# Which of two streams of matmul pieces goes on while a PSUM bank is half used, inside a state-space loop

## The chip, the cores and the metric

The kernel runs on one core of a Trainium2 chip. A core has five engines with queues of their own: TensorE (PE in the profile, with PEld for its weight loads), VectorE (DVE), ScalarE (ACT), GpSimd (POOL) and SyncE (SP), which here issues most DMAs. Matmuls write to PSUM, a small memory of eight banks; the other engines work mostly in SBUF. Each engine runs its own instructions in a fixed order, and waits on semaphores for the others. The metric is device time in microseconds; a kernel that computes the same in less time is better.

## The reference

A two-layer network on x of 64 sequences, 64 positions and 256 features, with a conditioning vector for each sequence. Each layer is a conditioning block, a mixing block, a second conditioning block and a feed-forward block, with two residual additions. The change touches the mixing block of the second layer, a selective state-space model, and what runs beside it, the shared experts and the router of the next block:

```
xz = x @ W_in;  xi, z = split(xz)                      # 512 + 512 channels
xc = silu(causal_conv4(xi) + b_conv)
delta_lr, B, C = split(xc @ W_xproj, [16, 32])         # 16 states
delta = softplus(delta_lr @ W_dt + b_dt);  A = -exp(A_log)
h_t = exp(delta * A) * h_(t-1) + delta * B * xc        # for each channel and state
y_t = sum over states of h_t * C + D * xc
x   = x + (y * silu(z)) @ W_out
...
shared = sum over 2 experts of (silu(x @ s_w1.T) * (x @ s_w3.T)) @ s_w2.T
scores = sigmoid([x, t_emb] @ W_router.T);  top 2 of 8 routed experts
```

Everything is float32.

## The kernel before

The kernel is one program for one core, written in Python against a layer that records the instructions, schedules them by priority and places the semaphores. The order in which the Python code issues an instruction is its priority; an instruction that asks for a buffer of a pool that has none free is put behind the one that frees it.

The 4096 tokens are handled in eight chunks of 512 (`CH`), each of eight sequences. Features lie on partitions, tokens along the free dimension. The state-space block is the function `mamba`. Its 512 channels are four tiles of 128 partitions, taken two at a time (`PI = 2`), and the 16 states are taken one after the other. So a chunk has 2 x 16 = 32 steps (`STEPS`), and the loop `for s in range(LAST)` has 256 steps. One step is, for one state and 2 x 512 columns:

- POOL: `hb = dx * B` (L1046, in `inputs`), issued two steps ahead. There are five `hb` buffers, and B comes by a broadcast DMA (L993) for two states at a time.
- ScalarE: the decay `dA = exp(A * delta)` (L1053, in `decay`), two instructions, issued one step ahead. There are three `dA` buffers, in PSUM.
- TensorE: `cb` (L998, in `spread_c`), which copies the row of C to all partitions; one PSUM bank.
- VectorE: two scans over time (L1094), which turn `hb` into the state, and a product with `cb` (L1096).
- TensorE: eight transposes (L1109) that add the 16 states up in two PSUM banks `yp0` and `yp1`.

Beside these steps runs all other work of the block, cut into pieces by Python generators:

- `head(c + 1)`: the input projection, convolution and delta of the next chunk (L919, L923, L926, L930, L934, L958 to L972).
- `gates(c, i0)`: the projection of z and its Silu (L982, L985, L988). In each tile the two halves of the sum over features are two pieces.
- `finish`: the transposes back (L1006, L1008, L1009).
- `project(c)`: the output projection (L1023, four matmuls for each of two tiles, in pairs), the residual addition that reads the bank (L1026), the load and the store of x (L1016, L1028). Its last act is to hand the new x to `beside`.
- `beside(c)`: router scores and shared experts of the next block for chunk c (L1499 to L1515, L1820 to L1842), up to 56 pieces a chunk. They use a bank of their own, `mq`.

The first four ask for one PSUM bank, `mp`, of which there is one during the loop. A generator that stops while it is in the middle of filling the bank yields `MID`; at the end of a use it yields nothing (`None`). Two streams stand in line: `urgent` (the `finish` and `project` of the chunk just scanned) and `pieces` (gates and the next chunk's head):

```
pieces = chain(pieces, gates(c, now, 0), islice(ahead, 3 * NI + PI + 4), gates(c, now, PI), ahead)
...
urgent = chain(urgent, finish(c, now, p * PI, yT))
if j == STEPS - 1:
    urgent = chain(urgent, project(c, now))
```

The function `turn` hands out one piece. It is called 40 times a chunk (`LEFT`), and more often where the next chunk's delta is needed sooner. After it, each step takes its share of `beside`. The `project` of a chunk runs in the first steps of the next one, where `pieces` begins with that chunk's gates.

On ScalarE the exponential, the logarithm and Silu need different function tables. Where two instructions that follow each other need different ones, a table load stands between them; it has the line of the instruction that needs it.

After the loop comes the stage of the routed experts (`mixtures`), with the rest of the shared experts for the last chunk.

Of the kernel before, what the change touches and what calls it, by code (L numbers as in the profile page):

```python
# [857 lines left out]
MID, END = "mid", "end"  # L858


def mamba(g, w, hs, beside):
# [16 lines left out]
    with (  # L878
# [97 lines left out]
        def gates(c, v, i0):  # L976
            sz = p2.tile([P, PI, CH], F32, name="sz")
            v.sz.append(sz)
            for i in range(PI):
                ps = one()  # L980
                for k in range(KD):
                    nc.tensor.matmul(ps, w.Win[:, k, ts(NI + i0 + i, P)], hs2[:, k, ts(c, CH)], start=(k == 0), stop=(k == KD - 1))  # L982
                    if k == 0:
                        yield MID
                nc.scalar.copy(sz[:, i, :], ps)  # L985
                if i < PI - 1:
                    yield
            nc.scalar.activation(sz, sz, AF.Silu)  # L988
            yield
# [11 lines left out]
        def finish(c, v, i0, yT):  # L1001

            for i in range(PI):
                ps = one()
                for t in range(CH // P):
                    nc.tensor.transpose(ps[:, ts(t, P)], yT[i][:, t, :], g.ident)  # L1006
                y = v.xc[:, i0 + i, :]
                nc.vector.scalar_tensor_tensor(y, y, w.col[:, 2, i0 + i : i0 + i + 1], ps, ALU.mult, ALU.add)  # L1008
                nc.gpsimd.tensor_mul(y, y, v.sz[i0 // PI][:, i, :])  # L1009
                yield  # L1010

        def project(c, v):

            nonlocal others
            x = p2.tile([P, KD, CH], F32, name="x")
            nc.sync.dma_start(x, g.x[:, :, ts(c, CH)])  # L1016

            to = x if c + 1 < NCH else hs2[:, :, :CH]
            yield
            for k in range(KD):  # L1020
                ps = one()
                for i in range(NI):
                    nc.tensor.matmul(ps, w.Wout[:, i, ts(k, P)], v.xc[:, i, :], start=(i == 0), stop=(i == NI - 1))  # L1023
                    if i % 2 and i < NI - 1:
                        yield MID
                nc.vector.tensor_add(to[:, k, :], x[:, k, :], ps)  # L1026
                yield
            nc.sync.dma_start(g.x[:, :, ts(c, CH)], to)  # L1028
            if c + 1 < NCH:
                for _ in others:  # L1030
                    pass
                others = beside(c, x)
# [36 lines left out]
        urgent, pieces, others = iter(()), iter(()), iter(())  # L1069
        mid = None  # L1070

        def turn():

            nonlocal mid
            got = next(pieces, None) if mid else next(urgent, END)
            if got is END:
                got = next(pieces, None)
            mid = got

        for s in range(LAST):  # L1080
            c, j = divmod(s, STEPS)
# [2 lines left out]
            if j == 0:  # L1084
                ahead = head(c + 1, vs[c + 1]) if c + 1 < NCH else iter(())
                pieces = chain(pieces, gates(c, now, 0), islice(ahead, 3 * NI + PI + 4), gates(c, now, PI), ahead)
# [11 lines left out]
            if s + AHEAD < LAST:  # L1098
                ca, ja = divmod(s + AHEAD, STEPS)
                while vs[ca].ready <= ja // S * PI:  # L1100
                    turn()
                inputs(s + AHEAD)
# [15 lines left out]
            if n == S - 1:  # L1118
# [3 lines left out]
# [3 lines that stand above are left out]
            while left < (j + 1) * LEFT // STEPS:  # L1125
                left += 1
                turn()
# [1061 lines left out]
```

## Time and profile before

| what | time, us |
|---|---|
| median of 3 runs | 2806.84 (2806.24 to 2814.49) |
| the profiled execution | 2807.03 |
| its span, first to last instruction | 2804.6 |
| before the state loop (0 to 698.5) | 698.5 |
| state loop (698.5 to 1849.1) | 1150.6 |
| after it | 955.5 |

Busy time over the whole span is 2339.3 us on PE, 1770.7 on DVE, 1375.5 on ACT and 1340.5 on POOL. In the state loop alone PE is busy for 924.1, DVE for 1013.0, ACT for 736.8 and POOL for 868.5 of the 1150.6 us.

In the profile each group of instructions is a line of the kernel, an engine, an operation, the tiles written and read, and a shape. "Idle before" is the time in which that engine did nothing before these instructions, and the name after the arrow is what ended it. A float32 matmul of the program shows as two instructions in the trace. Lines are those of the kernel before; in the changed kernel everything after `turn` stands four lines lower. The state loop's steps are counted from 0 in each chunk, and chunks from 0.

### The profile page before, as it was taken

The page shows a single profiled execution, that of the slowest core. Times are in us where ns is not written, and L with a number is a line of the kernel's source. Part 1 is how long each engine was busy: PE and PEld are TensorE (multiplying, and loading weights), DVE is VectorE, ACT ScalarE, POOL GpSimd, SP SyncE. Part 2 cuts the span into 40 slices and gives each one's busy share as a digit, 9 for nine tenths or more (in the row PEclk, how much of TensorE's full clock was granted, in tenths as well). Part 3 has the DMA queues.
Part 4 walks back from the last instruction along what each step waited for, and adds up shares of the span by engine and source line. Part 5 has one row for each costly group of instructions (what it writes and reads, how often), then busy time and mean ns, then how long its engine had stood idle before and what let it go on. Part 6 is the DMA issues. An engine that isn't in the chain of part 4 may idle for free.

```text
span 2804.6 us, 34388 instructions
## 1 busy us (share of the span) xinstructions
PE 2339.3 (83%) x11977; PEld 1674.0 (60%) x11996; DVE 1770.7 (63%) x2980; ACT 1375.5 (49%) x2289; POOL 1340.5 (48%) x1166
## 2 busy tenths in 40 slices
PE   3989967996568888887978888687786989999995
PEld 3634436773345555554655555566664768888884
DVE  0477748973999898888889797852353442322333
ACT  0567528885466757584757676533232222222220
POOL 0022345521696868685878787835555331111110
PEclk9979988997769999998999999899998999999997
DMA  9999820002112122221121222325685755555655
GB/s 224 372 358 347 276 70 1 1 1 90 68 68 83 65 74 70 72 72 57 65 92 67 83 81 75 106 70 178 212 287 194 278 216 206 214 192 197 227 192 189
DMA packets 180501, 406.03 MB, mean 145 GB/s; under 512 B 24785, under 2 KB 84434, under 8 KB 174946
## 3 DMA queue, kind: packets, MB, share of 16 engines
q1 hardware_dynamic: 166882, 366.80, 38.4%
q0 software_dynamic: 13440, 36.98, 3.4%
q8 instruction: 96, 1.57, 0.2%
q14 instruction: 83, 0.68, 0.1%
HBM read 280.76 MB, written 144.98 MB: 152 GB/s over the span
## 4 chain that ended last, share of the span: by engine, by line
PE 43%; DVE 21%; ACT 13%; issue 9%; POOL 5%; another core or an unknown queue 2%; DMA 1%; DVEq 0%; SPq 0%; ACTq 0%; POOLq 0%
DVE hb L1094 12%; PE ps L1684 11%; PE acc L1582 8%; PE out L450 4%; DVE hb L1096 3%; ACT dA L1053 2%; PE ps L1651 2%; PE yp L1109 2%; PE mq L1820 1%; DVE xc L926 1%; PE s L416 1%; PE acc L441 1%; ACT L1053 1%; PE mp L982 1%
## 5 line engine op out<-in xcount | busy, mean ns | idle before, releaser
L1046 POOL TENSOR_TENSOR hb<-dx,Bn 128x1024 f32<-128x1024 f32 x256 | 606.4, 2377 | 269.0 <-PE yp L1109 219.7
L1094 DVE TENSOR_TENSOR_SCAN hb<-dA,hb 128x512 f32<-128x512 f32 x512 | 602.1, 1210 | 63.2 <-ACT dA L1053 59.8
L1053 ACT ACTIVATE dA<-delta,negA 128x504 f32<-128x504 f32 x512 | 345.6, 685 | 303.5 <-DVE hb L1094 298.3
L1109 PEld LDWEIGHTS yp<-ident,hb 128*128 128x128 f32 x2048 | 264.4, 150 | 160.2 <-issue 121.2
L1096 DVE TENSOR_TENSOR hb<-hb,cb 128x1024 f32<-128x1024 f32 x256 | 312.4, 1220 | 66.3 <-PE cb L998 48.0
L1684 PE MATMUL ps<-gxT,w 128*128 128x256 f32 (+1 forms) x1600 | 324.5, 361 | 1.2 <-DVE gxT L1559 0.8
L1684 PEld LDWEIGHTS ps<-gxT,w 128*128 128x128 f32 x1600 | 276.3, 190 | 47.2 <-issue 12.4
L1820 PE MATMUL mq<-x,moe_s 128*128 128x256 f32 x896 | 244.5, 405 | 66.1 <-ACT up L1827 29.9
L1109 PE MATMUL yp<-ident,hb 128*128 128x128 f32 x2048 | 298.6, 290 | 0.0
L1358 POOL DMA_INDIRECT ffn_y<-gy,to x72 | 69.2, 962 | 432.3 <-ACT gy L1584 419.8
L1820 PEld LDWEIGHTS mq<-x,moe_s 128*128 128x128 f32 x896 | 166.6, 200 | 131.7 <-ACT sh L1824 42.5
L1688 DVE TENSOR_TENSOR gh<-gs,ps 128x256 f32<-128x256 f32 (+1 forms) x200 | 78.6, 394 | 213.5 <-ACT gs L1687 206.2
L1582 PE MATMUL acc<-w,gh 128*128 128x256 f32 (+1 forms) x864 | 190.0, 390 | 0.0
L1584 ACT ACTIVATE gy<-acc,wt 128x256 f32<-128x256 f32 x152 | 67.4, 474 | 246.8 <-PE acc L1582 227.5
L1687 ACT ACTIVATE gs<-ps 128x256 f32<-128x256 f32 (+1 forms) x200 | 72.4, 364 | 235.4 <-PE ps L1684 219.3
L998 PE MATMUL cb<-parts,pick 80*128 80x512 bf16 x256 | 104.5, 408 | 88.2 <-DVE hb L1096 83.9
L1582 PEld LDWEIGHTS acc<-w,gh 128*128 128x128 f32 (+1 forms) x864 | 146.8, 191 | 30.4 <-issue 13.2
L432 POOL TENSOR_TENSOR E<-E,z 128x1024 f32<-128x1024 f32 x32 | 61.6, 1925 | 194.5 <-DVE z L431 118.0
L1358 POOL DMA_INDIRECT moe_y<-gy,to x80 | 78.0, 975 | 110.2 <-ACT gy L1584 91.3
L1582 PE MATMUL acc<-w,rh 128*128 128x256 f32 x320 | 88.5, 419 | 45.6 <-ACT rh L1653 40.3
L1572 DVE TENSOR_REDUCE wt<-pick 128x2 f32<-128x4 f32 (+1 forms) x88 | 13.6, 156 | 174.7 <-ACT gy L1584 164.0
L450 PE MATMUL out<-oT,hs 128*128 128x512 f32 x256 | 117.8, 604 | 1.5 <-ACT oT L443 1.5
(470 smaller groups left out, 4457.1 us busy)
## 6 DMA issues: line engine op xcount, KB each, us to landing
w<-ffn_w SPq DMA_DIRECT2D x40, 2176.0 KB
Bn<-B SPq DMA_DIRECT2D x128, 512.0 KB
moe_x<-fill SPq DMA_DIRECT2D x130, 260.0 KB
ffn_x<-fill SPq DMA_DIRECT2D x129, 260.0 KB
w<-moe_w SPq DMA_DIRECT2D x48, 512.0 KB
ffn_w<-in_ffn_W_dram SPq DMA_DIRECT2D x16, 640.0 KB
gx<-moe_x SPq DMA_DIRECT2D x32, 260.0 KB
gx<-ffn_x SPq DMA_DIRECT2D x32, 260.0 KB
```

Of the source, the lines that this page charges most:

```text
L450: nc.tensor.matmul(ps, M[:, o, ts(k, P)], v.o[:, o], start=(o == 0), stop=(o == H // 2 - 1))
L998: nc.tensor.matmul(t, pick[:, n : n + 1].to_broadcast([rows, P]), v.parts, start=True, stop=True)
L1046: nc.gpsimd.tensor_mul(hb, vs[c].dx[p], Bn[:, n % NB, :].unsqueeze(1).to_broadcast([P, PI, CH]))
L1053: nc.scalar.activation(decays[s][i][:, :, 1:], seq(vs[c].delta[p][:, i, :])[:, :, 1:], AF.Exp, scale=A[:, p * PI + i, n : n + 1],)
L1094: ins = nc.vector.tensor_tensor_scan(h, dA[i].rearrange("p b l -> p (b l)"), h, 0.0, ALU.mult, ALU.add)
L1096: ins = nc.vector.tensor_tensor(hb, hb, cb.unsqueeze(1).to_broadcast([P, PI, CH]), ALU.mult)
L1109: nc.tensor.matmul(yp[i][:, t, :], hb[:, i, ts(t, P)], g.ident, start=(n == 0 and t == 0), stop=(n == S - 1 and t == CH // P - 1), is_tran ...
L1358: i = self.g.nc.gpsimd.indirect_dma_start(out=self.y, out_offset=bass.IndirectOffsetOnAxis(ap=to, axis=0), in_=y, in_offset=None)
L1582: nc.tensor.matmul(po[s], h, w, start=(i == 0), stop=(i == n - 1))
L1684: nc.tensor.matmul(ps[:, j, :], v.w12[:, k, ts(j * (full + 1) + i, P)], v.xT[:, k, :], start=(k == 0), stop=(k == KD - 1))
L1688: nc.vector.tensor_mul(v.h[:, i, : v.rows], s, ps[:, 1, :])
L1820: nc.tensor.matmul(ps[:, i % 2, :], w[:, k, ts(i, P)], xu[:, k, :], start=(k == 0), stop=(k == KD - 1))
```

## The change

Only `turn` is changed. Before, it remembered what the last piece had yielded: after a `MID`, from either stream, the next piece came from `pieces`. After, it remembers the stream itself: after a `MID` the next piece comes from the stream that yielded it.

```diff
@@ -1072,10 +1072,14 @@
         def turn():
 
             nonlocal mid
-            got = next(pieces, None) if mid else next(urgent, END)
-            if got is END:
-                got = next(pieces, None)
-            mid = got
+            if mid is None:
+                mid = urgent
+            got = next(mid, END)
+            if got is END and mid is urgent:
+                mid = pieces
+                got = next(mid, END)
+            if got is not MID:
+                mid = None
```

`MID` is the string "mid" and `END` the string "end". The two differ where `urgent` yields `MID`, which only `project` does, once for each of its two tiles.

## The prediction

> **What bounds the kernel now.** I read the page first, then the stretches of the state loop by chunk, then VectorE's waits inside that loop, then the order of time around the longest of them. Of the page, the span and three groups:
>
> ```profile
> span 2804.6 us, 34388 instructions
> L1094 DVE TENSOR_TENSOR_SCAN hb<-dA,hb 128x512 f32<-128x512 f32 x512 | 602.1, 1210 | 63.2 <-ACT dA L1053 59.8
> L1053 ACT ACTIVATE dA<-delta,negA 128x504 f32<-128x504 f32 x512 | 345.6, 685 | 303.5 <-DVE hb L1094 298.3
> L1096 DVE TENSOR_TENSOR hb<-hb,cb 128x1024 f32<-128x1024 f32 x256 | 312.4, 1220 | 66.3 <-PE cb L998 48.0
> ```
>
> The scan and its product are the state loop. VectorE's idle time before them has two main releasers: ScalarE's decay (59.8 us) and TensorE's row copy of C, `cb` (48.0). By stretches (us, then busy time and count of PE, PEld, DVE, ACT, POOL, the granted clock, DMA):
>
> ```profile
> core 0: us, PE busy (x) PEld busy (x) DVE busy (x) ACT busy (x) POOL busy (x), PEclk, DMA share, GB/s
> ...
> 1113.60:1256.60 143.00, 123.02 (x574) 82.80 (x573) 124.69 (x118) 96.46 (x132) 108.44 (x53) 0.96 0.21 71
> 1256.60:1414.60 158.00, 125.89 (x556) 82.88 (x555) 135.76 (x151) 98.60 (x133) 107.92 (x56) 0.89 0.18 61
> ...
> 1849.10:1869.30 20.20, 18.94 (x73) 12.48 (x73) 2.87 (x4) 2.50 (x5) 7.33 (x27) 1.00 0.27 83
> 1869.30:2804.60 935.30, 828.42 (x4077) 683.27 (x4077) 337.13 (x1372) 223.74 (x524) 260.26 (x290) 0.94 0.60 212
> ```
>
> The first two rows are chunks 3 and 4 of eight: VectorE is the fullest engine, and the rest of the chunk is its waiting. After 1849 PE is. So a wait of VectorE removed in the loop shortens the run, and nothing later absorbs it except PE's own backlog. VectorE's waits between 698 and 1845 us:
>
> ```profile
> engine line waited for: us in total, times, longest us
> DVE hb L1094 <- ACT dA L1053: 59.8, 38, 7.6
> DVE hb L1096 <- PE cb L998: 48.0, 34, 4.9
> ```
>
> And the sixth step of chunk 3:
>
> ```profile
> 1131.77 1.22 DVE L1096 TENSOR_TENSOR hb<-hb,cb 128x1024 f32<-128x1024 f32 x1
> ...
> 1132.91 2.33 DVE L1094 TENSOR_TENSOR_SCAN hb<-dA,hb 128x512 f32<-128x512 f32 x2
> ...
> 1135.16 0.66 DVE L1026 TENSOR_TENSOR x<-x,mp 128x512 f32<-128x512 f32 x1
> ...
> 1135.87 2.99 PE L982 MATMUL mp<-hs,Win 128*128 128x512 f32 x4 [2.55 <-DVE x L1026]
> ...
> 1138.66 1.75 PE L1836 MATMUL mq<-moe_s,sh 128*128 128x256 f32 x4
> ...
> 1140.25 0.38 PE L998 MATMUL cb<-parts,pick 80*128 80x512 bf16 x1
> ...
> 1140.67 1.22 DVE L1096 TENSOR_TENSOR hb<-hb,cb 128x1024 f32<-128x1024 f32 x1 [4.85 <-PE cb L998]
> ```
>
> The first half of the output projection (L1023) fills the bank `mp`; L1026 empties it, but stands behind two scans. The gate's L982 wants the same bank, stands in PE's queue before `cb`, and so `cb` comes 4.85 us late. A step without waits is 3.57 us (1132.91 less 1129.34, the start of the scans before).
>
> **What the change does to the order.** Before, a MID from `project` sent the next turn to `pieces`, which asked for the bank that `project` was filling. In the built order of the changed kernel the four pairs of L1023 stand in three or four consecutive steps, and the gates follow. No matmul, activation, vector operation or DMA is added or removed, except table loads on ScalarE: 11 more (L1053 46 to 52, L1831 13 to 16, L930 5 to 8, L988 16 to 15). `beside(c)` starts two to three steps earlier, since `project` ends earlier.
>
> **The sum.**
>
> 1. *Collisions removed.* VectorE's `cb` waits where L982 stood behind L1026: 4.9, 4.8, 3.2, 3.2, 1.9, 4.1, 4.0 us in chunks 2 to 7 (chunk 6 has two): 26.1. Chunk 1 had none.
>
> 2. *What stands there now.* After the second L1026 PE runs one half of the gate (two passes, 1.02), both score matmuls (L1499, 1.02 each, so 1.9 pipelined) and `cb` (0.42): 3.4 us. VectorE wants it after a product and two scans, 1.22 + 2.33 = 3.55. I take 0.2 in each of seven chunks, +1.4. L982 ran at a clock of 0.61 in one of these places (2.99 us for x4) and at 1.00 in another (1.98 at 1278.51); at the low clock the 2.9 us become 4.6 and the wait 1.7, which makes the bounds 0 and +12. L1023's second pairs wait for L1026 too, but only 1.9 us of matmul follow before `cb`: hidden.
>
> 3. *Scores.* L1511 waits for L1505, which stands behind two scans, and `cb` behind L1511: 0.8, 0.8, 0.8, 1.8 and 2.6 before, 6.8 in all. Now L1505 stands a product and two scans earlier, but a gate half and four L1820 pairs follow L1511 ahead of `cb`: 0.05 + 0.41 + 1.02 + 2.0 + 0.42 = 3.9 against 3.55, 0.35 each, seven times 2.5. So -4.3; bounds -6.8, and +8.6 if each costs 2.2, the mean of the two long ones.
>
> 4. *ScalarE.* For each step I add up its work from the rows (two decays 1.38; table load 1.28; Silu 1.91 or 1.06; copies 0.58; L959 and L960 0.69, L962 1.06, L963 and L964 1.15, L969 1.06) and subtract 3.57 plus VectorE's other work of the step (L926 0.72, L1008 0.74, L1026 0.66). ScalarE may be ahead by at most the three decay buffers; where the lead is used up, the rest is a wait. With a largest lead of 8.0 us, which I chose because it gives the measured waits, the old order gives 5.8, 7.9, 7.9, 12.0, 4.7, 10.8, 6.5 for chunks 1 to 7 (55.5), measured 6.0, 8.1, 8.1, 10.4, 5.2, 10.0, 10.2. The new order gives 10.6, 10.6, 10.6, 5.9, 9.3, 9.3, 1.0: 57.3. So +1.6 (to its rounding). In chunks 1 to 3 two Silu now fall on either side of the logarithm (step 26 of the chunk costs 6.3), where before two shared one load in step 30 (2.8); chunk 4 and the first steps of chunks 6 and 7 lose a pair of loads, and step 30 of chunks 5 and 6 gets one. Of the 11 loads (14.1 us of ScalarE) nearly all fall where ScalarE only waits for scans (298.3 us, above). That is their cover; bare, they cost +14.1. The other bound is -8, if chunk 1 to 3 stay as before.
>
> A rule against this: the Trainium skill, "ScalarE: Activation LUTs", section "What ACT_TABLE_LOAD costs", gives a switch 1283 ns and a drain of about 1380. By it the 11 loads would be 29 us (an estimate) and eat the whole gain. In the trace the load is 1.283 us and the activation behind it starts at once (load at 1153.43, Silu at 1154.72), so no drain shows and the row decides.
>
> 5. *The tail.* From the last state transposes (1849.1) to the first matmul of the next stage (1869.3) are 20.2 us. Eight L1820 (1.03 for two) and four of sixteen L1836 (7.07 for all) leave it, 5.9 us of PE. But the last transposes now have four L1836 ahead of them that wait for POOL's product. SP's weight loads, which stood before the store of the shared rows (L1842), now stand behind it. I take -3, bounds 0 and -5.9.
>
> 6. *Moved with it.* The x store of `project` (L1028) goes three steps earlier on SP, past one or two B loads (L993), and the x load (L1016) stays; SP's B loads wait for POOL's buffers (935.0 us), POOL's product never waits for a B load, so nothing. POOL's list keeps its work. The other 15.1 us of `cb` waits (48.0 less 26.1 and 6.8) come from the `beside` groups; their neighbours change everywhere. I take +5, since groups now stand behind ScalarE's bursts; bounds -5 and +15.
>
> Sum: -26.1 + 1.4 - 4.3 + 1.6 - 3 + 5 = -25.4. The profiled execution took 2807.0 (span 2804.6), 0.2 from the median 2806.84. Forecast **2782 us**.
>
> **Rivals.**
>
> *ScalarE takes the place (slower).* Step 30 of chunk 4 has two Silu loads in one step and costs 7.6. The new order has such a pair in five chunks (step 26 of 1, 2, 3; step 30 of 5, 6). If each costs 7.6 on top of the old waits, +38.0: -26.1 + 1.4 - 4.3 - 3 + 5 + 38.0 = +11, 2818. It decides from where the old waits of steps 29 to 32 do not go. For: ScalarE's exponentials and logarithm stay there. Against: the pair in step 30 of chunks 1 to 3 is gone from the order. Chance 0.10.
>
> *The loads are uncovered and `beside` collides elsewhere (no change).* +14.1 for 1.6 and +15 for 5: -26.1 + 1.4 - 4.3 + 14.1 + 15 = 0, tail lost too: 2807. For: the neighbours of all 56 `beside` pieces of a chunk shift. Against: the lead of 8. Chance 0.10.
>
> *The bank wait stays at half.* Low clock at the new place (+12), scores keep 6.8: -26.1 + 12 + 1.6 - 3 + 5 = -10.5, 2796. For: PE idles some 1.4 us before L982, and 2.55 us was enough for the low clock. Chance 0.17. "TensorE: Matmul & The Clock Gate", Part 1, lets the clock fall only after an idle window of about 3.4 us; by it there would be no loss here, an estimate of 2784 for this rival. The row shows 0.61 after 2.55 us, so I keep the price.
>
> *It doesn't do what it says.* The built order shows L1023 unbroken by gates in all of chunks 1 to 7; chance under 0.02, 2807.
>
> **How the numbers follow.** Forecast 0.59, better than the good bounds 0.03, half 0.17, no change 0.11, slower 0.10. What a measurement of this kernel can tell from no change is 0.3%, 8.4 us. So faster 0.79, same 0.11, slower 0.10. Low end: -26.1 - 6.8 - 5.9 - 5 and no new costs is 2763. The high end 2804 leaves the slower rival and most of no change outside.
>
> **What would show it.** L982's wait for L1026 (21.5 us on PE) shrinks to about 1.4 us a chunk, and no `cb` wait above 3 us remains in the first ten steps of a chunk. Chunks 2 and 3 fall from 143 us to some 138; chunk 1 grows by some 4; chunk 7 falls by ten. ScalarE's table loads rise by 14 us, its decay waits stay near 60. Wrong if decay waits exceed 75, or if `cb` waits stay above 40 with other neighbours.

## The result, and the profile after

The changed kernel takes 2806.3 us (median of 20 runs, 2800.2 to 2814.9), the kernel before 2809.9 on the same chip (20 runs, 2794.3 to 2816.5). The ratio is 0.9996 with a 95% interval of 0.9985 to 1.0008: no difference that can be measured. The forecast was 2782 us, and the time lies above its range of 2763 to 2804 us too. The profiled execution of the changed kernel took 2811.2 us, 4.9 above its median, with a span of 2809.1; its state loop is 1154.3 us long against 1147.1 in the profile before (first scan to last product).

The page of the changed kernel, with the span and the three groups that were shown of before:

```profile
span 2809.1 us, 34414 instructions
...
L1098 DVE TENSOR_TENSOR_SCAN hb<-dA,hb 128x512 f32<-128x512 f32 x512 | 601.6, 1208 | 65.6 <-ACT dA L1053 65.4
L1053 ACT ACTIVATE dA<-delta,negA 128x504 f32<-128x504 f32 x512 | 345.0, 683 | 300.9 <-DVE hb L1098 299.0
...
L1100 DVE TENSOR_TENSOR hb<-hb,cb 128x1024 f32<-128x1024 f32 x256 | 311.9, 1218 | 60.2 <-PE cb L998 43.9
```

VectorE's work in these groups is as long as before; the waits have only changed places: 5.6 us more for decays, 4.1 us less for `cb`. The same stretches as before, chunks 3 and 4, the tail from the last state transposes to the next stage, and that stage:

```profile
core 0: us, PE busy (x) PEld busy (x) DVE busy (x) ACT busy (x) POOL busy (x), PEclk, DMA share, GB/s
1120.20:1266.60 146.40, 125.78 (x568) 83.56 (x568) 124.37 (x119) 99.00 (x134) 108.60 (x53) 0.93 0.20 69
1266.60:1418.60 152.00, 122.44 (x550) 79.58 (x549) 134.43 (x151) 98.08 (x134) 108.36 (x57) 0.91 0.20 66
1854.30:1868.20 13.90, 13.16 (x49) 7.89 (x47) 2.87 (x4) 1.29 (x3) 3.69 (x24) 1.00 0.04 11
1868.20:2809.10 940.90, 830.05 (x4077) 684.41 (x4077) 340.19 (x1372) 222.84 (x524) 259.37 (x290) 0.94 0.60 212
```

Chunk 3 grew from 143.0 to 146.4 us, chunk 4 fell from 158.0 to 152.0. VectorE is busy for the same time in both (124.7 and 124.4 in chunk 3), so the difference is all waiting. VectorE's longest waits in the loop, by what ended them:

```profile
engine line waited for: us in total, times, longest us
DVE hb L1098 <- ACT dA L1053: 65.4, 38, 7.6
DVE hb L1100 <- PE cb L998: 43.9, 36, 4.1
DVE x L1026 <- PE mp L1023: 9.0, 6, 3.1
```

The third line is new. The same view of TensorE tells what became of the collision. First the kernel before, then the changed one:

```profile
PE mp L982 <- DVE x L1026: 21.5, 14, 2.5
...
PE mp L1023 <- POOL xc L1009: 1.1, 1, 1.1
```

```profile
PE mp L1023 <- POOL xc L1009: 12.4, 8, 2.4
...
PE mp L982 <- DVE x L1026: 3.4, 4, 1.6
```

The gate's wait for L1026 is nearly gone, as the change means it to be. In its place `project` itself waits, for GpSimd's product L1009.

To see where the waits went, I added up VectorE's idle time in each of the 256 steps, by what ended it and by the part of the chunk (us, all eight chunks):

| waits of VectorE | before | after |
|---|---|---|
| steps 0 to 8: `cb` and `mp` | 26.0 | 28.4 |
| steps 9 to 19: `cb` and `mp` | 16.5 | 3.8 |
| steps 20 to 31: `cb` and `mp` | 8.6 | 21.3 |
| decays, whole loop | 59.9 | 65.4 |

Three things have to be explained: why the first nine steps gained nothing although the collisions are gone, what is new in steps 20 to 31, and why the decays cost more.

### The profile page after: what moved, and what is told of

Its sections match the earlier page's. It is cut to its first block, busy times and chain, and to the rows that moved or that the text cites. A ratio compares the mean times of both kernels' runs of the same rounds, so it can differ in the third digit from the quotient of the medians.

```text
span 2809.1 us, 34414 instructions
## 1 busy us (share of the span) xinstructions
PE 2345.4 (83%) x11977; PEld 1679.9 (60%) x11996; DVE 1774.8 (63%) x2980; ACT 1386.3 (49%) x2300; POOL 1338.6 (48%) x1166
## 4 chain that ended last, share of the span: by engine, by line
PE 45%; DVE 17%; ACT 10%; issue 10%; POOL 9%; DMA 1%; another core or an unknown queue 1%; SPq 0%; DVEq 0%; ACTq 0%; POOLq 0%
PE ps L1688 11%; DVE hb L1098 9%; PE acc L1586 9%; PE out L450 4%; PE mq L1824 2%; DVE hb L1100 2%; PE yp L1113 2%; POOL hb L1046 2%; PE ps L1655 2%; ACT dA L1053 2%; PE mp L1023 1%; PE s L416 1%; PE acc L441 1%; PE ps L1696 1%
## 5 line engine op out<-in xcount | busy, mean ns | idle before, releaser
L1046 POOL TENSOR_TENSOR hb<-dx,Bn 128x1024 f32<-128x1024 f32 x256 | 605.9, 2373 | 263.8 <-PE yp L1113 209.5
L1098 DVE TENSOR_TENSOR_SCAN hb<-dA,hb 128x512 f32<-128x512 f32 x512 | 601.6, 1208 | 65.6 <-ACT dA L1053 65.4
L1100 DVE TENSOR_TENSOR hb<-hb,cb 128x1024 f32<-128x1024 f32 x256 | 311.9, 1218 | 60.2 <-PE cb L998 43.9
L1688 PEld LDWEIGHTS ps<-gxT,w 128*128 128x128 f32 x1600 | 276.3, 190 | 47.4 <-issue 12.4
L1113 PE MATMUL yp<-ident,hb 128*128 128x128 f32 x2048 | 304.5, 293 | 0.0
L1824 PE MATMUL mq<-x,moe_s 128*128 128x256 f32 x896 | 250.4, 413 | 56.4 <-ACT up L1831 27.1
L1588 ACT ACTIVATE gy<-acc,wt 128x256 f32<-128x256 f32 x152 | 67.1, 472 | 250.7 <-PE acc L1586 227.9
L1576 DVE TENSOR_REDUCE wt<-pick 128x2 f32<-128x4 f32 (+1 forms) x88 | 13.6, 155 | 174.2 <-ACT gy L1588 158.0
```

Source lines behind the costliest of these rows:

```text
L1046: nc.gpsimd.tensor_mul(hb, vs[c].dx[p], Bn[:, n % NB, :].unsqueeze(1).to_broadcast([P, PI, CH]))
L1098: ins = nc.vector.tensor_tensor_scan(h, dA[i].rearrange("p b l -> p (b l)"), h, 0.0, ALU.mult, ALU.add)
L1100: ins = nc.vector.tensor_tensor(hb, hb, cb.unsqueeze(1).to_broadcast([P, PI, CH]), ALU.mult)
L1113: nc.tensor.matmul(yp[i][:, t, :], hb[:, i, ts(t, P)], g.ident, start=(n == 0 and t == 0), stop=(n == S - 1 and t == CH // P - 1), is_tran ...
L1688: nc.tensor.matmul(ps[:, j, :], v.w12[:, k, ts(j * (full + 1) + i, P)], v.xT[:, k, :], start=(k == 0), stop=(k == KD - 1))
L1824: nc.tensor.matmul(ps[:, i % 2, :], w[:, k, ts(i, P)], xu[:, k, :], start=(k == 0), stop=(k == KD - 1))
```

## The experiments

Comparisons are with runs of the kernel before on the same chip, since chips differ by some 50 us. In the tables below "first steps" are the waits for `cb` and `mp` in steps 0 to 8, "last steps" those in steps 20 to 31, both read from one profiled execution as above. Two executions of the same instructions differ there: chunks 1 to 3 are built alike in two of the kernels below, and their last steps had 4.1, 0.9 and 4.0 us in one and 4.1, 0.8 and 1.8 in the other.

### Where `beside` stands

In the changed kernel `project` ends at step 4 and not at step 7, so `beside` begins three steps, or five pieces, earlier. Theory A says that this is what spent the gain; theory B, that the loop has another bound. The first run delays `beside` again, the second gives the old kernel the early `beside`:

```diff
-                others = beside(c, x)
+                others = chain(repeat(None, 5), beside(c, x))
```

> The changed kernel, with five empty places put in front of the pieces of `beside`, so that the router's and shared expert's work stands at about the steps where it stood in the kernel before. Theory A (the collisions on `mp` are gone as forecast, and their 26 us are spent again because `beside` now runs about three steps earlier, so that its matmuls on the bank `mq` and its Silu meet the head's chain of Exp, Ln and copies in steps 21 to 26): clearly faster than the kernel before, by 15 to 25 us (2785 to 2795), VectorE's waits for `cb` in the loop at 25 us or less against 48.0 before and 43.9 in the changed kernel; table loads 117 as before, waits for decays 50 to 60. Theory B (the loop is bound by something else, for example ScalarE's or GpSimd's work per chunk, and a wait removed at one place comes up at another whatever is done): within 5 us of the kernel before, sum of VectorE's two kinds of waits unchanged at about 105 to 110 us.

```diff
                 others = beside(c, x)
+                for _ in range(5):
+                    next(others, None)
```

> The kernel before, with the first five pieces of `beside` issued at once when `project` ends: `beside` stands about as early as in the changed kernel, but the hand-out still asks for `mp` in the middle of its use. Theory A: slower than before by 10 to 25 us, since it has both the collisions and the new waits in steps 21 to 26; waits for `cb` 60 us or more. Theory B: within 5 us of before.

| run | ratio to before, 95% | loop | first steps | last steps | decays |
|---|---|---|---|---|---|
| five places later | 0.9958 (0.9942 to 0.9973) | 1135.5 | 27.8 | 7.5 | 59.8 |
| old hand-out, five earlier | 1.0026 (1.0015 to 1.0037) | 1157.4 | 27.8 | 9.2 | 68.1 |

Theory B fell: the kernel with `beside` put back is faster than the kernel before, by 11.5 us (2743.4 against 2754.9). Theory A holds in this run for the last steps and the decays, which are back at their old length (7.5 and 59.8; the trace has 116 table loads, as many as the kernel before). But it forecast 15 to 25 us, and the first nine steps still wait 27.8 us. In the second run the decays rise to 68.1, but the waits for `cb` stay at 48.2 where I had written 60 or more, the last steps stay at 9.2, and it loses 8 us of the 10 to 25. So with the old hand-out an early `beside` lengthens the decays, but not the last steps.

What an early `beside` does in the last steps of the changed kernel is seen in its chunk 3, steps 22 to 24:

```profile
1213.88 1.47 PE L1824 MATMUL mq<-x,moe_s 128*128 128x256 f32 x4 [2.50 <-ACT sh L1828]
...
1215.28 2.07 PE L958 MATMUL mp<-dbc,Wdt 16*128 16x512 f32 x2
...
1217.93 1.22 DVE L1100 TENSOR_TENSOR hb<-hb,cb 128x1024 f32<-128x1024 f32 x1 [0.98 <-PE cb L998]
...
1224.07 1.22 DVE L1100 TENSOR_TENSOR hb<-hb,cb 128x1024 f32<-128x1024 f32 x1 [2.67 <-PE cb L998]
...
1229.86 1.22 DVE L1100 TENSOR_TENSOR hb<-hb,cb 128x1024 f32<-128x1024 f32 x1 [2.32 <-PE cb L998]
```

TensorE waits 2.50 us for ScalarE to copy the bank `mq` away; after that the granted clock is low (0.59 between 1212 and 1226, 1.00 in the seven microseconds before), two matmuls of L958 take 2.07 us where two of 512 columns take 1.02 at full clock, and three `cb` in a row come late.

### More delay, and what piles up at the end of `project`

The same edit with 10 and 20 empty places. By a running sum of ScalarE's work these should have cut the decays' waits.

> As the first run, with ten empty places: `beside` some three steps later than in the kernel before. Theory A: it too is faster than the kernel before, how much depends on what it meets there; a running sum of ScalarE's work per step gives 48 us of waits for decays against 56 with five empty places, so some 5 to 10 us faster than that run. Theory B: no change.

> As the first run, with twenty empty places, so that the shared expert's pieces lie in the last steps of a chunk and in the first of the next. Theory A: the running sum of ScalarE's work gives only 20 us of waits for decays, 36 less than with five places, so up to 30 us faster than that run, if what is still left of `beside` at the end of `project` (it is issued there at once) does not cost it. Theory B: no change.

| run | ratio, 95% | loop | first steps | last steps | decays |
|---|---|---|---|---|---|
| 10 places | 1.0109 (1.0093 to 1.0126) | 1168.1 | 59.4 | 5.0 | 52.1 |
| 20 places | 1.0156 (1.0139 to 1.0173) | 1175.3 | 59.9 | 6.8 | 32.4 |

The decays fell (to 52.1 and 32.4, where the running sum gave 48 and 20), and both kernels are slower all the same: a second miss for theory A. What is left of `beside` when `project` ends is issued there at once, and it is 5 to 12 pieces with ten places and 15 to 22 with twenty. With twenty, steps 9 to 19, which the table leaves out, wait another 36 us (4 with ten). The longest of these waits, in step 9 of chunk 7:

```profile
1770.03 2.78 PE L1840 MATMUL mq<-moe_s,sh 128*128 128x256 f32 x12
...
1773.05 4.58 PE L1840 MATMUL mq<-moe_s,sh 128*128 128x256 f32 x20 [0.24 <-POOL sh L1832]
...
1778.75 1.22 DVE L1100 TENSOR_TENSOR hb<-hb,cb 128x1024 f32<-128x1024 f32 x1 [12.16 <-PE cb L998]
```

Hardly anything is waited for between these lines: TensorE has 32 matmul instructions of L1840 in front of one `cb`. From this came theory C: a step of VectorE needs 3.57 us, and whatever TensorE has beyond that between two `cb` is a wait. The next four runs take the pile away (`others` is no longer emptied at the end of `project`), with five and three empty places; or, with no empty places, hold `beside` back at the start of a chunk. The two begin at step 4 and at step 7, so that the 56 pieces go into 28 and 25 steps.

```diff
-                for _ in others:
-                    pass
-                others = beside(c, x)
+                others = chain(
+                    others,
+                    chain(repeat(None, 5), beside(c, x)))
```

> As the first run (five empty places), but what is left of `beside` when `project` ends is no longer issued there at once: it goes on with the same rate, and the next chunk's pieces come after it. Theory C, formed from the first four runs (a step of VectorE needs 3.57 us, and a wait for `cb` arises wherever TensorE has more than that queued between two `cb`; the collision on `mp` was only part of such a wait): no step of chunk 6 and 7 has 9.2 or 7.5 us of matmuls in front of `cb` any more, VectorE's waits for `cb` and `mp` in steps 0 to 8 fall from 28 us to about 20 to 24, and ScalarE's running sum falls from 56 to 43: 5 to 15 us faster than the first run, ratio to the kernel before 0.990 to 0.994. Theory A (what counts is only where `beside` meets the head): as the first run, 0.996.

> As the run above with three empty places in place of five. Theory C: TensorE's sum over 3.57 us is 25 us against 32 there, ScalarE's running sum 40 against 43: some 5 to 10 us faster than that run. Theory A: slower than with five, since `beside` meets the head's chain earlier; between the changed kernel and the first run, 0.997 to 0.999.

```diff
-            for _ in range((j + 1) * most // STEPS - j * most // STEPS):
+            for _ in range(max(0, j - 3) * most // 28 - max(0, j - 4) * most // 28):
```

> No empty places and nothing issued at once, but no piece of `beside` is handed out in the first three steps of a chunk, where TensorE has `finish` and `project`; the same 56 pieces go into the other 29 steps. Theory C: TensorE's sum over 3.57 us is 13 us, the least of all these kernels, nearly nothing of it in steps 0 to 8, so waits for `cb` and `mp` in steps 0 to 8 below 12 us against 28; with ScalarE's running sum at 53 the ratio is 0.985 to 0.992. Theory A: `beside` meets the head's chain about as in the changed kernel, 0.997 to 1.000.

> As the run above, with nothing handed out in the first six steps of a chunk, so that `beside` begins at step 7 and stands where it stood in the kernel before, at a closer spacing. Theory C: waits for `cb` and `mp` in steps 0 to 8 below 8 us; TensorE's sum over 3.57 us 25 us, most of it now in steps 18 to 31; ScalarE's running sum 49: ratio 0.985 to 0.992. Theory A: as the first run or a little better, 0.993 to 0.996.

"Behind it" is the time from the end of the loop's last product to the end of the span.

| run | ratio, 95% | loop | behind it | first steps (`cb` + `mp`) | last steps | decays |
|---|---|---|---|---|---|---|
| no pile, 5 places | 1.0027 (1.0014 to 1.0039) | 1131.0 | 924.4 | 12.3 + 8.9 | 5.8 | 55.5 |
| no pile, 3 places | 0.9971 (0.9957 to 0.9984) | 1134.1 | 915.2 | 11.2 + 4.0 | 13.8 | 57.3 |
| held to step 4 | 0.9975 (0.9963 to 0.9988) | 1146.4 | 902.6 | 7.3 + 12.4 | 14.2 | 68.0 |
| held to step 7 | 1.0085 (1.0072 to 1.0098) | 1170.0 | 904.1 | 3.2 + 12.2 | 29.2 | 78.1 |

The first row has a loop 16 us shorter than before, and its first steps fell to 21.2 us, where 20 to 24 was forecast; but the pieces put off stood behind the loop, which is 20 us longer there (904.0 with the pile), and the ratio of 0.990 to 0.994 that theory C forecast was missed. By their ratios the second and the third row lie where theory A had them (0.997 to 0.999, and 0.997 to 1.000), not where theory C had them. The two that hold `beside` back show where theory C stops: `cb` nearly stops waiting (7.3 and 3.2), but `mp` has 12 us, and the first steps stay at 19.7 and 15.4, not below 12 and 8. With less in TensorE's queue it reached L1023 sooner and stood there, 18.1 and 10.5 us in all for GpSimd's L1009. Its clock was lower as well: in the first nine steps of chunks 2 to 4 the granted clock was 0.83 in the run held to step 4 and 0.82 to 0.87 in the other, against 0.95 and 0.96 in the changed kernel.

### TensorE's load by itself

Both kernels without most of the shared expert's second product, which lies mostly in the first steps (the kernel before stands for both here):

```diff
-                    nc.tensor.matmul(ps[:, t, :], h[:, i, ts(t, P)], self.s2[:, i, :], start=(i == 0), stop=(i == NS - 1))
+                    if i in (0, NS - 1): nc.tensor.matmul(ps[:, t, :], h[:, i, ts(t, P)], self.s2[:, i, :], start=(i == 0), stop=(i == NS - 1))
```

> The kernel before, with 192 of the 256 matmuls of the shared expert's second product (L1836) left out: of the eight that are summed, the first and the last are kept, so its output is not the reference's. Everything else, the hand-out of pieces too, stays. Theory C (TensorE's work between two `cb` makes most of the wait, the bank `mp` the rest): the waits for `cb` in steps 0 to 8 fall from 25.9 us to 12 to 16, about what TensorE stood idle for L1026 at the collisions (12.8 us). Theory A (the whole of these waits is the bank's): they stay at 20 us or more, less only the 1.75 us of L1836 behind L982 in some of them.

> The changed kernel with the same 192 matmuls left out. Theory C: the waits for `cb` in steps 0 to 8 fall from 19.4 us to below 5 (those of chunks 6 and 7, 7.0 and 7.9 us, nearly to nothing), the waits for `mp`, where TensorE waits for GpSimd's product L1009, stay at 9 us or more; and against the run above the change is now worth something, 5 to 10 us of the loop. Theory A: the waits for `cb` in steps 0 to 8 stay, since no bank is freed sooner, and the two light kernels differ as little as the full ones.

Theory C missed both times. The waits for `cb` in steps 0 to 8 were 21.8 us in the first (12 to 16 forecast; theory A's 20 or more was met) and 14.7 in the second (below 5 forecast), with 12.3 more for `mp`. And the light changed kernel is slower than the light kernel before, 2781.3 against 2769.2 us; its decays wait 67.1 against 48.9. The pair does not test the load alone, however. The matmuls that are left ran at a lower clock: in the first nine steps of chunks 2 to 4 the granted clock was 0.82, 0.88 and 0.88 in the light changed kernel, where the full one had 0.96, 0.95 and 0.96, and in chunk 2 its 137 matmuls took 33.3 us where 145 took 31.6. How much of the waits is this clock, and why the decays differ by so much, stays open. What TensorE waited for in the light kernels was GpSimd and what hangs on it: in the kernel before at the start of chunk 2, 4.36 us for the shared expert's product L1828, with a `cb` wait of 7.05 us behind it.

### GpSimd

In the first 20 us of chunk 6 of the changed kernel GpSimd is full:

```profile
core 0: us, PE busy (x) PEld busy (x) DVE busy (x) ACT busy (x) POOL busy (x), PEclk, DMA share, GB/s
1559.20:1579.20 20.00, 15.67 (x76) 11.70 (x75) 15.63 (x15) 9.03 (x15) 19.92 (x12) 0.91 0.22 79
1579.20:1599.20 20.00, 18.49 (x87) 11.76 (x87) 15.33 (x16) 7.10 (x12) 9.82 (x5) 1.00 0.26 93
```

It has the rest of the head (L970 to L972, 2.36 us each), one L1046 of 2.35 in every step, L1009 and L1832. How that meets `project` is seen in chunk 2:

```profile
985.76 2.34 POOL L1046 TENSOR_TENSOR hb<-dx,Bn 128x1024 f32<-128x1024 f32 x1
...
985.85 1.13 PE L1023 MATMUL mp<-xc,mWout 128*128 128x512 f32 x2 [1.28 <-POOL xc L1009]
...
988.06 1.26 POOL L1009 TENSOR_TENSOR xc<-xc,sz 128x512 f32<-128x512 f32 x1
...
989.38 2.07 PE L1023 MATMUL mp<-xc,mWout 128*128 128x512 f32 x2 [2.40 <-POOL xc L1009]
...
991.49 0.69 DVE L1026 TENSOR_TENSOR x<-x,mp 128x512 f32<-128x512 f32 x1 [3.10 <-PE mp L1023]
```

The second L1009 stands behind an L1046 on GpSimd, L1023's last pair waits 2.40 us for it, and L1026, which stands in VectorE's queue in front of the next product, waits 3.10. The pair also runs at half clock, 2.07 us where two such passes take 1.02 at full clock. In the changed kernel such a stretch of low clock begins in step 2 or 3 of chunks 2, 3, 4, 6 and 7; two of the five, with the granted clock in the third column from the end:

```profile
989.30:992.70 3.40, 3.32 (x8) 1.91 (x9) 1.21 (x2) 0.00 (x0) 2.33 (x2) 0.50 0.74 228
1716.30:1719.70 3.40, 3.40 (x11) 2.83 (x12) 1.14 (x2) 0.69 (x1) 3.40 (x3) 0.50 0.02 5
```

Before the change TensorE waited for L1009 only once in the loop, for 1.1 us. The new hand-out by itself does not bring this wait; the early `beside` does. With `beside` put back by five places TensorE's wait for L1009 is small, and with the old hand-out and an early `beside` it is nearly that of the changed kernel (12.4 us). The two runs in this order:

```profile
PE mp L1023 <- POOL xc L1009: 2.5, 4, 1.1
```

```profile
PE mp L1023 <- POOL xc L1009: 11.2, 7, 2.4
```

Theory D: GpSimd takes the place of the bank. Four runs leave its products out of both kernels, first L1009 alone, then the shared expert's (L1828, in the changed kernel L1832) as well; their output is not the reference's:

```diff
-                nc.gpsimd.tensor_mul(y, y, v.sz[i0 // PI][:, i, :])
```

> The kernel before without the product by the gate (L1009, GpSimd, four of 1.27 us in a chunk); the output is not the reference's. Theory D, formed from the light runs (in the first steps of a chunk GpSimd is full with the head's last L970 to L972, the inputs L1046, L1009 and the shared expert's L1828, so TensorE waits for it, and a bank that comes free sooner is only taken into a longer wait for GpSimd): little changes here, the waits for `cb` and `mp` in steps 0 to 8 stay within 6 us of the 26.0 before. Theory C (TensorE's load alone): within 6 us too.

> The changed kernel without the product L1009. Theory D: TensorE's wait of L1023 for L1009 (12.4 us) is gone, VectorE's waits for `mp` in steps 0 to 8 fall from 9.0 us to 3 or less, and the loop is shorter by 5 to 12 us, so that the change comes out 3 to 10 us better against the run above than the changed kernel against the kernel before. Theory C: the matmuls still have to be done, so what `mp` loses `cb` gains, and the loop stays within 4 us.

```diff
-                            nc.gpsimd.tensor_mul(to, to, up)
```

> The kernel before without L1009 and without the shared expert's product L1828 on GpSimd (eight more of 1.27 us in a chunk). Theory D: the collisions on `mp` stay, so the waits for `cb` and `mp` in steps 0 to 8 are 15 us or more. Theory C: they stay at 22 to 28 us.

> The changed kernel without L1009 and L1832. Theory D: the waits for `cb` in steps 2 and 3 of chunks 6 and 7 (4.3 and 5.3 us), where TensorE waits for a copy that waits for L1832, go too, so the waits for `cb` and `mp` in steps 0 to 8 fall from 28.4 us to 14 or less, and against the run above the change is worth 5 to 15 us in the loop's first steps. Theory C: 22 us or more are left.

The first row is from the chip of the result; on the chip of the other two the kernel before took 2805.7 us.

| GpSimd's products | before, us | changed, us | first steps before | first steps changed | loop before | loop changed |
|---|---|---|---|---|---|---|
| all | 2809.9 | 2806.3 | 26.0 | 28.4 | 1147.1 | 1154.3 |
| without L1009 | 2808.4 | 2793.6 | 26.5 | 21.2 | 1144.4 | 1139.8 |
| and without L1828/L1832 | 2809.5 | 2790.9 | 25.4 | 12.5 | 1143.6 | 1131.4 |

Theory D holds for the changed kernel as it stands: the kernel before doesn't feel the missing work (its ratios are 1.0007 and 1.0013), since its first steps wait for the bank; the changed kernel does (0.9961, 0.9946 to 0.9975, and 0.9947, 0.9926 to 0.9967). Of the 22.9 us by which its loop is shorter without both products, 15.9 are in the first steps and 6.8 in the last ones. VectorE's own instructions are no shorter (the scans take 618.3 and 618.5 us in all), so it is waiting that went. Without L1009 TensorE's wait for it and most of VectorE's waits for `mp` go:

```profile
DVE hb L1098 <- ACT dA L1053: 66.6, 37, 7.6
DVE hb L1100 <- PE cb L998: 35.0, 29, 4.0
...
DVE x L1026 <- PE mp L1023: 2.5, 3, 0.8
```

9.0 us became 2.5. The low clock goes too. Without both products the granted clock is 1.00 in the first nine steps of each of chunks 2 to 7; the last of them:

```profile
1690.20:1730.20 40.00, 35.76 (x177) 23.85 (x175) 34.30 (x33) 18.54 (x32) 27.58 (x15) 1.00 0.33 109
```

So these runs take away the waits for GpSimd and the low clock together, and do not say how much is which. With both products out, the change is worth 12.9 us in the first steps (25.4 less 12.5). TensorE stood idle for L1026 at the seven collisions for 2.20, 2.55, 2.20, 0.68, 1.21, 2.18 and 1.79 us, in all 12.8. That the two agree so well is partly chance, since one of the seven (2.18) lies in step 9.

### A version that beats both

Nothing piled up, and the pieces handed out fast enough from chunk 4 on that none is left behind the loop:

```diff
-            most = BESIDE if c + 1 < NCH else BESIDE_LAST
+            most = (56 if c < 4 else 64) if c + 1 < NCH else 72
```

> As the run with five empty places and nothing issued at once, but from chunk 4 on `beside` gets 64 pieces a chunk and not 56, so that no backlog is left behind the loop. Theory C: the loop as there or better (1131 us; TensorE's sum over 3.57 us 24 against 32), and the part behind the loop back from 922 to 902 us: about 2735 us, ratio to the kernel before 0.991 to 0.995.

With three empty places, and 62 pieces:

> As the run above with three empty places, and 62 pieces a chunk from chunk 4 on. Theory C: TensorE's sum over 3.57 us 20, ScalarE's running sum 47, both about as above: ratio 0.991 to 0.996, the part behind the loop at 902 us.

The old hand-out with 62 pieces and no pile, as a control; and 60 pieces:

> The kernel before with what the best version so far has beside the change: nothing of `beside` issued at once, and 62 pieces a chunk from chunk 4 on; no empty places, since its `project` ends three steps later anyway. If the change itself is worth something once `beside` stands right, this stays within 0.3% of the kernel before (0.997 to 1.003), with the collisions' waits of 25 us in steps 0 to 8. If the gain of the best version (0.993) came from the rate alone, 0.992 to 0.996.

> As the best version so far (three empty places, nothing issued at once), with 60 pieces a chunk from chunk 4 on and not 62: just enough for the 57, 61 and 59 pieces and empty places of chunks 4 to 6. Waits for `cb` in steps 20 to 31 of chunks 4 to 6 (15.3 us) should fall by half, as the groups stand further apart: 0 to 8 us faster than that version, ratio 0.990 to 0.994.

| run | ratio, 95% | loop | first steps | last steps | decays |
|---|---|---|---|---|---|
| 5 places, 64 | 0.9944 (0.9922 to 0.9966) | 1131.8 | 20.0 | 12.2 | 59.7 |
| 3 places, 62 | 0.9928 (0.9912 to 0.9944) | 1127.3 | 9.9 | 23.2 | 55.8 |
| old hand-out, 62 | 1.0063 (1.0049 to 1.0077) | 1163.3 | 33.0 | 20.3 | 66.1 |
| 3 places, 60 | 0.9985 (0.9971 to 0.9998) | 1148.6 | 22.4 | 23.6 | 64.9 |

Three places with 62 pieces is the best of all: 2784.1 us against 2805.9 for the kernel before on its chip. TensorE's waits there, in the loop:

```profile
PE mp L1023 <- POOL xc L1009: 6.1, 5, 2.3
...
PE mp L982 <- DVE x L1026: 2.0, 2, 1.6
```

The control shows that the rate alone loses 16 us (0.997 to 1.003 had been forecast), so the gain comes from the change and the setting of `beside` together. Other settings of `beside` with the old hand-out were not run. The last run shows how narrow this is: two pieces a chunk fewer, and chunks 6 and 7 have 5.4 and 9.8 us in their first steps, where the best version has 0.8 and 1.5. The last steps, which I expected to be halved, stayed.

## Why the prediction was wrong, step by step

**Step 1, collisions removed (-26.1): the mechanism right, the price too high.** The gates hardly wait any more (TensorE's 21.5 us for L1026 are 3.4). But I took the whole of VectorE's wait for `cb` as the bank's. TensorE stood idle for the bank for only part of it, and the row that I showed had it: 2.55 us of a wait of 4.85. Over the seven places that is 12.8 of 26.1. In the rest TensorE works on the matmuls of that step, which have to be done all the same; in the chunk that I showed it was busy for 123.0 us and VectorE for 124.7. This division is read from the traces; the 12.9 us of the runs without GpSimd's products fit it.

**Step 2, what stands there now (+1.4, bounds 0 to +12): this step failed.** The first nine steps had 4.0 us of other waits before (26.0 less the 22.0 of the collisions there) and have 28.4 now: 24.4 new, twice the upper bound. I counted only the matmuls that TensorE has behind L1026. I had noted that `beside` starts earlier, but gave that no price in these steps, and I did not ask what else the pairs of L1023 need. They need L1009 from GpSimd, which is full at the start of a chunk; with `beside` moved forward TensorE gets there before GpSimd has it, waits, and then runs at half clock. The four runs without GpSimd's products show the size: of the 28.4 us they take away 7.2 (L1009) and 8.7 more (L1832), the low clock with them. The 12.5 left hold the 4.0 of before and some 8.5, within the bounds that I had given, which by elimination I put down to TensorE's own load. With `beside` put back, as in the first experiment, the wait for L1009 is small and the first steps wait 27.8 us all the same; 6.6 of that goes with the pile (21.2 without it), and what makes up the rest stays open. My rival "the bank wait stays at half" had the right size for step 1, and the low clock that it expected at the new place is there: 0.50 for 3.4 us in five chunks, by an estimate some 1.7 us of TensorE's time each. What it did not have is the wait for GpSimd ahead of it.

**Step 3, scores (-4.3).** 6.8 us in steps 9 and 10 became 3.6 (1.2 in each of chunks 1 to 3): -3.2.

**Step 4, ScalarE (+1.6, bounds -8 to +14.1): right within its bounds.** Measured +5.6 (59.8 to 65.4), with 127 table loads for 116, the 11 more that I had counted. So the loads were mostly covered. The rival that ScalarE takes the place is excluded; its bound of 75 us for the decays was not reached.

**Step 5, the tail (-3, bounds 0 and -5.9): right in direction, at the edge of its bounds.** From the last state transposes, as I had counted, to the next stage's first scores it took 20.2 us and takes 13.9: -6.3. But these transposes now end later behind the last product. From the end of that product it took 22.3 us and takes 17.3, and this -5.0 is what adds to the loop's waits.

**Step 6, the rest (+5, bounds -5 and +15): within its bounds by luck, as the difference of two large parts.** The last steps gained 12.7 us of `cb` waits, and what was neither score nor collision in steps 9 to 19 lost 5.4 (5.6 to 0.2): +7.3. I had named the changed neighbours of the `beside` pieces, but not the mechanism. In the place shown, TensorE waits for the copy of `mq`, which stands on ScalarE behind the head's copies and decays, and then runs at the low clock. The first run shows that in the changed kernel this needs the early `beside`: put back by five pieces, the last steps are at 7.5 us. It is not the only condition, since with the old hand-out and an early `beside` they are at 9.2.

By what was measured: -26.1 + 24.4 - 3.2 + 5.6 + 7.3 = +8.0 for the loop's waits (the loop grew by 7.2) and -5.0 in the tail, +3.0 in one pair of executions; the medians differ by -3.6, with an interval that holds nought. So it ended nearest the rival "no change". That had `beside` colliding elsewhere right, but took the other half from uncovered loads, where it was mostly GpSimd. Of what I said would show it, chunks 2 and 3 went to 146 and not to 138, and two `cb` waits above 3 us are left in the first ten steps (3.1 and 3.2, in chunks 6 and 7); and the sign that I had named for a wrong forecast, waits for `cb` above 40 us with other neighbours, is there with 43.9.

## What to carry to other kernels

A wait behind a collision need not be the price of the collision. Here the idle time of the engine that collides (TensorE's 12.8 us) fitted what the change was worth better than the wait of the one at the end of the chain (26.1). Then ask for everything that the freed work needs next, on every engine: here an operand from an engine that is full in that stretch took the place of the bank, and the wait for it brought a low clock. And a stream that ends sooner starts its successor sooner; compare the two with the successor put back to its old place before you judge the change.

## What the runs showed of the hardware

TensorE's clock fell behind short gaps: behind 2.50 us of idle time in the changed kernel the granted clock was 0.59 between 1212 and 1226, and eight transposes took 1.91 us for 1.04. The Trainium skill, "TensorE: Matmul & The Clock Gate", Part 1, speaks of an idle window of about 3.4 us; here the low clock stood behind shorter gaps, as at the collision of 2.55 us in the prediction. The length of the gap alone does not decide it: in the kernel before, behind two collisions of 2.20 us each, the clock was 0.50 in chunk 2 (993.4 to 996.7) and 1.00 in chunk 4 (1278.5 to 1281.9).

GpSimd's product of 128x512 floats took 1.26 us, where VectorE's addition of the same shape (L1026) took 0.66: 1.9 times. The Trainium skill, "Trainium Architecture — The Big Picture", section "The five engines, in one table", has it two times slower, which agrees.

The same kernel before took 2755 to 2756 us on some chips and 2806 to 2810 on others. Chunk 0, which is alike in all the kernels run here, took 134.7 to 135.5 us on both; the part behind the loop, which differs a little between these kernels, took 902 to 925 us on the first and 946 to 963 on the second. What makes them differ stays open.
